# Dividing the side work of an attention loop over two steps, the PSUM bank held between them

## Chip, cores and metric

The kernel runs on one core of one Trainium2 chip. The metric is the device time of one execution in microseconds; lower is better. TensorE is called PE here, VectorE DVE, ScalarE ACT, GpSimd POOL and SyncE SP, as in the profile.

## What is computed

One layer of masked graph attention with residual norms, on x of shape (F, N, C) = (8, 2048, 256) with H = 8 heads of D = 32 channels, in float32:

```python
qkv = einsum('fnc,ck->fnk', x, w_qkv); q, k, v = split(qkv, 3)        # heads of 32
scores = einsum('fnhd,fmhd->fhnm', q, k) / sqrt(D)
attn = softmax(where(adj > 0, scores, -1e9), axis=-1)                 # adj is (2048, 2048), shared by all f and heads
t = einsum('fhnm,fmhd->fnhd', attn, v).reshape(F, N, C)
x1 = layernorm(x + t)
h = relu(einsum('fnc,cd->fnd', x1, w1) + b1)
x2 = layernorm(x1 + einsum('fnd,dc->fnc', h, w2) + b2)
out = layernorm(x + x2)
```

## The kernel before, in words

**The main loop.** `items` is a list of 8 x 4 x 2 x 16 = 1024 steps (f, qc, g, mb): graph copy f, a chunk qc of 512 queries, a group g of four heads, and a block mb of 128 keys. Sixteen steps with the same (f, qc, g) are called a group below. In step t the kernel first lets side work advance (`advance`), then issues `scores(items[t + LEAD])` with LEAD = 2, then `values(items[t])`, then `add_up(items[t])`.

- `scores` (lines 202 to 215) computes four heads' scores for one key block: four matmuls on PE into two PSUM tiles of two banks each (`score_pair`, three such pairs in turn, six banks), two DVE instructions that add the mask and write half of an SBUF tile `p` each (line 213), and one ACT instruction that takes the exponential of all of `p` in place (line 215).
- `values` (line 227) multiplies the four heads of `p` with V into the group's accumulator `O`, one PSUM bank that is held for the whole group. After the last block ACT copies it out as `oT` (line 231).
- `add_up` (lines 240 to 247) sums the `p` tiles of a group for the softmax's denominator. Blocks 0, 3, 6, 8, 11, 13, 15 are summed on POOL into block 0's tile (line 247); blocks 1, 4, 7, 10 and blocks 2, 5, 9, 12 are summed by two chains of accumulating DMAs, issued from POOL, into block 1's and block 2's tile (line 244); block 14 stands alone. So four tiles of a group stay alive until `denominator` has read them. The pool `pp` has 10 buffers for `p`.

**The PSUM banks.** Six of the eight banks hold scores. Of the other two (`ps_x`), one is the accumulator `O` of the group that runs, and the other, `1 - state["side"]`, is the single bank for all side work. The two change roles at each group's first step. No side work is issued in that step (`if mb: advance(t, 1)`).

**The side work.** Everything else is written as Python generators: `turn` (transposes x and makes the queries), `project` (keys and V), `turn_mask` (transposes the mask, first f only), `denominator` (sums `p` over keys by matmuls with ones, lines 271 to 295), `outcome` (transposes and scales the result, adds x by an accumulating DMA), and `tail` (norms, the two feed-forward matmuls `w1s` at line 339 and `w2s` at line 349, more norms, the store). They wait in the list `fill`, sorted by a due time written out by hand (`NEXT`, `start`). A generator yields a positive number to pause for so many steps, `TURNED`, `ROOM` or an `INPUTS` code to wait for a buffer, and `BANK` before it takes the side bank. `advance(t, 1)` walks the list in order of due time and lets one job pass its `BANK` in each step. All the matmuls up to the next `yield` are then issued at once; below, these are a *piece*. A piece ends with an instruction on ACT or DVE that empties the bank. The pieces of before are:

| piece | matmuls on PE | emptied by |
|---|---|---|
| transposes of `turn`, `tail` (`turnT`, `yT`, lines 157, 328) | 4 of 128x128 | ACT |
| transposes of `denominator`, `outcome` (`denT`, `outT`, lines 288, 311) | 4 of 128x128 | DVE |
| transposes of the mask (line 132) | 8 in bf16 | DVE |
| `chan`: a query or key chunk (`channels`, line 171) | 2 of 128x512 | ACT |
| `V` (line 192) | 8 of 128x128 | ACT |
| `den`, twice for each group (line 281) | 8 of 32x512 | ACT, after the second |
| `w1` (line 339) | 2 of 128x512 | ACT |
| `w2` (line 349) | 4 of 128x256 | DVE |

`denominator` is the one job that keeps the bank over two of its pieces: it yields `BANK` between them, and is by its due time the first in the list when it does. Its first piece becomes possible four steps after the group's last one (`start(t + SUM, ...)` with SUM = 4), that is at block 3 of the next group.

If the step's coming scores need a V chunk that doesn't exist yet, the loop calls `advance` again until it does.

Of the kernel before, what the change touches and what calls it, by code (L numbers as in the profile page):

```python
# [10 lines left out]
F32 = mybir.dt.float32  # L11
# [7 lines left out]
P = 128  # L19
H = 8  # L20
D = 32
CH = 512
# [3 lines left out]

SUM_MIN = 1e-25
SUM_MAX = 1e19
BANK, TURNED, ROOM, INPUTS = -1, -2, -3, -10

MASKED = -57344.0

# [21 lines left out]
def fast_path(ctx, tc, cst, x, adj, out, RS):  # L54
    nc = tc.nc
    F, N, C = x.shape
    NCK, TPC, MB = N // CH, CH // P, N // P
# [5 lines left out]
    kp = ctx.enter_context(tc.tile_pool(name="kp", bufs=2 * NCK + 2))  # L63
    qp = ctx.enter_context(tc.tile_pool(name="qp", bufs=2 * NCK + 2))
# [10 lines left out]
    ctx.enter_context(tc.manual_schedule())  # L75

    ident, identb, wqkv, w1s, w2s = cst["ident"], cst["identb"], cst["wqkv"], cst["w1s"], cst["w2s"]
    state = {"pair": 0, "side": None, "turn": 0, "turned": False, "tails": 0}

    def score_pair():  # L80
        i = state["pair"]
# [16 lines left out]
    def take(shape, dt):  # L98
        live.pop(0)
        live.append(ld.tile(shape, dt, name="in"))  # L100
        return live[-1]

    def give(t):
        live[:] = [None if u is t else u for u in live]
# [39 lines left out]
    QT, KT, V, XT = {}, {}, {}, {}  # L144
# [3 lines left out]
    def turn(f, c):  # L148
        yield INPUTS - 2
        xc, xT = take([P, TPC, C], F32), take([P, 2, CH], F32)  # L150
        nc.sync.dma_start(xc, x[f, c * CH:(c + 1) * CH, :].rearrange("(j p) c -> p j c", p=P))
        yield 3
        for a in range(2):
            yield BANK
            ps = bank()
            for j in range(TPC):
                nc.tensor.transpose(ps[:, j * P:(j + 1) * P], xc[:, j, a * P:(a + 1) * P], ident)
            nc.scalar.copy(xT[:, a, :], ps)
        give(xc)
        nc.sync.dma_start(XD[f][c], xT)  # L160
        XT[f, c] = xT
        yield 1
        for g in range(2):
            yield BANK
            QT[f, c, g] = channels(qp, "qT", xT, g * P)
        give(xT)

    def channels(pool, name, xT, k0):
        ps = bank()
        for a in range(2):  # L170
            nc.tensor.matmul(ps, wqkv[:, a, k0:k0 + P], xT[:, a, :], start=(a == 0), stop=(a == 1))  # L171
        t = pool.tile([P, CH], F32, name=name)
        nc.scalar.copy(t, ps)  # L173
        return t

    def project(f, c, g, xT=None):
        if xT is None:
            while (f, c) not in XT:
                yield 1
            yield INPUTS - 1  # L180
            xT = take([P, 2, CH], F32)
            nc.sync.dma_start(xT, XD[f][c])
            yield 3
            while len(KT) < (2 * f + g) * NCK + c:
                yield 1
        yield BANK
        KT[f, c, g] = channels(kp, "kT", xT, C + g * P)
        yield BANK
        ps = bank()
        for j in range(TPC):  # L190
            for a in range(2):
                nc.tensor.matmul(ps[:, j * P:(j + 1) * P], xT[:, a, j * P:(j + 1) * P],  # L192
                                 wqkv[:, a, 2 * C + g * P:2 * C + (g + 1) * P], start=(a == 0), stop=(a == 1))
        v = vp.tile([P, TPC, P], F32, name="v")
        nc.scalar.copy(v, ps.rearrange("p (j c) -> p j c", c=P))
        V[f, c, g] = v
        give(xT)
# [19 lines left out]
    LAST = MB - 1  # L217
# [53 lines left out]
    def denominator(f, qc, g):  # L271
        grp = (f, qc, g)
        terms = [PT.pop((f, qc, g, ALONE))] + [PT.pop((f, qc, g, chain[0])) for chain in MOVED + (POOLED,)]
        yield BANK
        ps = bank()
        for n, term in enumerate(terms):
            if n == 2:
                yield BANK
            for h in range(4):
                r = D * h  # L280
                nc.tensor.matmul(ps[r:r + D, :], cst["ones"], term[:, h, :], start=(n == 0), stop=(n == 3))  # L281
        dT = op.tile([P, CH], F32, name="dT")
        nc.scalar.copy(dT, ps)
        yield 1
        yield BANK
        ps = bank()
        for j in range(TPC):
            nc.tensor.transpose(ps[:, j * P:(j + 1) * P], dT[:, j::TPC], ident)
        if g == 0:
            RC[f, qc] = op.tile([P, TPC, H], F32, name="rc")  # L290
        rc = RC[f, qc]
        den = ps.rearrange("p (j c) -> p j c", c=P)[:, :, ::D]
        nc.vector.reciprocal(rc[:, :, 4 * g:4 * g + 4], den)
        nc.vector.tensor_tensor(RS[:, 0], RS[:, 0], den, ALU.add)
        nc.vector.tensor_tensor(RS[:, 1], RS[:, 1], den, ALU.min)
        if g == 1:
            begin = items.index((f, qc, g, LAST)) + SUM + 2
            start(begin, outcome(f, qc), begin)
# [20 lines left out]
    def tail(f, qc, y, xin):  # L319
        yield from norm(y)  # L320
        yield TURNED
        state["turned"] = True
        yT = work.tile([P, 2, CH], F32, name="turned")
        for a in range(2):
            yield BANK
            ps = bank()
            for j in range(TPC):
                nc.tensor.transpose(ps[:, j * P:(j + 1) * P], y[:, j, a * P:(a + 1) * P], ident)  # L328
            nc.scalar.activation(yT[:, a, :], ps, AF.Identity, bias=cst["be1c"][:, a:a + 1], scale=cst["g1c"][:, a:a + 1])
        yield 1  # L330
        nc.gpsimd.tensor_tensor(y, y, rows(cst["g1r"]), ALU.mult)
        yield 1
        nc.gpsimd.tensor_tensor(y, y, rows(cst["be1b2r"]), ALU.add)
        hT = work.tile([P, 2, CH], F32, name="hT")
        for d in range(2):
            yield BANK
            ps = bank()
            for a in range(2):
                nc.tensor.matmul(ps, w1s[:, a, d * P:(d + 1) * P], yT[:, a, :], start=(a == 0), stop=(a == 1))  # L339
            nc.scalar.activation(hT[:, d, :], ps, AF.Relu, bias=cst["b1s"][:, d:d + 1], scale=1.0)  # L340
        state["turned"] = False
        yield 1
        z = y
        for jj in range(0, TPC, 2):
            yield BANK
            ps = bank()
            for j in range(jj, jj + 2):
                for d in range(2):
                    nc.tensor.matmul(ps[:, (j - jj) * C:(j - jj + 1) * C], hT[:, d, j * P:(j + 1) * P], w2s[:, d, :],  # L349
                                     start=(d == 0), stop=(d == 1))  # L350
            nc.vector.tensor_tensor(z[:, jj:jj + 2, :], ps.rearrange("p (b c) -> p b c", c=C), z[:, jj:jj + 2, :], ALU.add)  # L351
        yield 1
        yield from norm(z)
        nc.gpsimd.tensor_tensor(z, z, rows(cst["g2r"]), ALU.mult)  # L354
        yield 1
        nc.gpsimd.tensor_tensor(z, z, rows(cst["be2r"]), ALU.add)  # L356
        yield 1
        nc.gpsimd.dma_start(z, xin, accum_op=ALU.add)
        yield 7
        yield from norm(z)  # L360
        nc.sync.dma_start(out[f, qc * CH:(qc + 1) * CH, :].rearrange("(p j) c -> p j c", p=P), z)
        state["tails"] -= 1


    fill = []

    def start(t, gen, due):
        fill.append([t, gen, 1, due])
        fill.sort(key=lambda e: e[3])

    def advance(t, banks):
        inputs = True
        for e in list(fill):
            while e[0] <= t:
                if e[2] == BANK:
                    if not banks:
                        break
                    banks -= 1  # L380
                elif e[2] < INPUTS:
                    inputs = inputs and not any(u is not None for u in live[:INPUTS - e[2]])
                    if not inputs:
                        break
                elif e[2] == TURNED and state["turned"] or e[2] == ROOM and state["tails"] == 2:
                    break
                e[2] = next(e[1], None)
                if e[2] is None:
                    fill.remove(e)
                    break  # L390
                if e[2] > 0:
                    e[0] = t + e[2]

    def mask_ahead(qc):
        for mc in range(NCK):
# [22 lines left out]
    for t, (f, qc, g, mb) in enumerate(items):  # L418
# [8 lines left out]
                due = t + MB // 2 if what is turn else items.index((f + 1, 0, which[1], which[0] * TPC)) - LEAD - 1  # L427
                start(t, what(f + 1, *which), due)
        if mb:
            advance(t, 1)  # L430
        if t + LEAD < len(items):
            nf, _, ng, nmb = items[t + LEAD]
            t0 = t
            while (nf, nmb // TPC, ng) not in V:
                advance(t0, 1)
                t0 += 1
            scores(items[t + LEAD])
        values(items[t])
# [3 lines left out]
    t = len(items)  # L442
    while fill:
        t += 1
        advance(t, 1)


@with_exitstack
# [233 lines left out]
```

## Time and profile before

| | us |
|---|---|
| median of 3 runs | 3766.22 (3762.61 to 3768.49) |
| the profiled execution | 3763.43 |
| its span | 3761.7 |
| PE busy | 3244.8 |
| DVE busy | 2761.9 |
| POOL busy | 2594.1 |
| ACT busy | 2412.1 |

The span runs from the first instruction to the last. A busy PE means that matmuls were in flight, not that PE was at its peak; matmuls overlap, so the times of single ones add to more than the busy time. The granted TensorE clock was 0.974 of full speed in the mean. The profile's chain of work that ended last covers 1% of the span here and says nothing of the loop; the loop is read from the timeline, the waits and the groups.

### The profile page before, as it was taken

To read this page: it belongs to the slowest core of one execution; us is meant where nothing else is said; L and a number is where in the kernel's file an instruction comes from. 1 tells how busy PE (TensorE), PEld (TensorE's weight loads), DVE (VectorE), ACT (ScalarE), POOL (GpSimd) and SP (SyncE) were. 2 spreads that over 40 slices of the span, in tenths; PEclk is the share of its full clock that TensorE was granted. 3 is DMA by queue.
4 is the path that set the end of the run, shared out by engine and by line. 5 is a ranking of instruction groups with operands and counts; after the bars stand their busy time and mean duration, and the time that the engine had idled before them with its cause. 6 is when DMAs were issued, how large, how long until landed. Compare 5 with 4: busy or idle time off the path is not lost. (4 is left out here: it accounts for less than half of the span.)

```text
span 3761.7 us, 53803 instructions
## 1 busy us (share of the span) xinstructions
PE 3244.8 (86%) x22020; PEld 1044.6 (28%) x22020; DVE 2761.9 (73%) x3207; ACT 2412.1 (64%) x1921; POOL 2594.1 (69%) x1355
## 2 busy tenths in 40 slices
PE   6778788988988989888998899888898888988884
PEld 4222223222322223222332223222232222322221
DVE  1886776777678776888667876787767777688882
ACT  2555655667667666666667765676766676677663
POOL 0555666677677776777757876677767777687775
PEclk8899999999999999999999999999999999999997
DMA  4665767677767767666757876766676676677663
GB/s 150 153 156 131 169 153 166 132 160 164 163 135 168 163 145 180 140 154 149 183 135 153 180 150 153 155 152 153 151 179 138 149 174 148 161 157 145 143 136 75
DMA packets 115181, 573.84 MB, mean 153 GB/s; under 512 B 11632, under 2 KB 29168, under 8 KB 61680
## 3 DMA queue, kind: packets, MB, share of 16 engines
q0 software_dynamic: 64512, 436.24, 57.6%
q1 hardware_dynamic: 48064, 132.13, 10.1%
q8 instruction: 174, 2.85, 0.3%
q10 hardware_dynamic: 2352, 1.97, 0.2%
q14 instruction: 79, 0.65, 0.1%
HBM read 129.90 MB, written 37.75 MB: 45 GB/s over the span
## 5 line engine op out<-in xcount | busy, mean ns | idle before, releaser
L213 DVE TENSOR_TENSOR p<-s,mask 128x1024 f32<-128x1024 f32 x2048 | 2408.8, 1218 | 751.4 <-PE s L210 482.0
L215 ACT ACTIVATE p<-p 128x2048 f32<-128x2048 f32 x1024 | 1957.0, 1911 | 1214.6 <-DVE p L213 878.9
L247 POOL TENSOR_TENSOR p<-p 128x2048 f32<-128x2048 f32 x384 | 1835.8, 4819 | 664.5 <-ACT p L215 656.2
L210 PE MATMUL s<-qT,kT 32*128 32x512 f32 x8192 | 1186.0, 649 | 236.3 <-DVE p L213 235.9
L227 PE MATMUL x<-p,v 128*32 128x512 f32 x8192 | 1110.0, 614 | 0.0
L244 POOL DMA_DIRECT2D p<-p x384 | 381.2, 1012 | 367.1 <-ACT p L215 143.6
L210 PEld LDWEIGHTS s<-qT,kT 32*128 32x128 f32 x8192 | 323.6, 185 | 855.9 <-DVE p L213 700.0
L227 PEld LDWEIGHTS x<-p,v 128*32 128x32 f32 x8192 | 162.1, 108 | 790.7 <-issue 629.9
L171 PE MATMUL x<-in,wqkv 128*128 128x512 f32 x476 | 238.0, 623 | 22.9 <-ACT oT L231 10.2
L265 ACT ACTIVATE y<-y,nb,rs 128x256 f32<-128x256 f32 x384 | 224.9, 589 | 39.9 <-POOL nb L262 39.9
L281 PE MATMUL x<-p,ones 128*32 128x512 f32 x2048 | 245.1, 597 | 2.3 <-DVE y L351 0.9
L254 DVE BATCH_NORM_STATS2 st<-y 128x6 f32<-128x256 f32 x384 | 159.8, 416 | 26.7 <-DMA y<-in_x_dram 26.7
L349 PE MATMUL x<-w2s,hT 128*128 128x256 f32 x512 | 129.4, 396 | 45.6 <-ACT oT L231 42.3
L339 PE MATMUL x<-turned,w1s 128*128 128x512 f32 x256 | 130.6, 633 | 20.7 <-ACT hT L340 19.3
L171 PEld LDWEIGHTS x<-in,wqkv 128*128 128x128 f32 x476 | 82.4, 192 | 185.5 <-issue 72.1
L192 PE MATMUL x<-wqkv,in 128*128 128x128 f32 x960 | 123.0, 281 | 6.4 <-ACT kT L173 6.3
L192 PEld LDWEIGHTS x<-wqkv,in 128*128 128x128 f32 x960 | 112.5, 192 | 57.4 <-ACT kT L173 34.0
L349 PEld LDWEIGHTS x<-w2s,hT 128*128 128x128 f32 x512 | 93.1, 192 | 113.4 <-ACT oT L231 68.6
L351 DVE TENSOR_TENSOR y<-x,y 128x512 f32<-128x512 f32 x64 | 44.2, 691 | 98.5 <-PE x L349 97.8
L281 PEld LDWEIGHTS x<-p,ones 128*32 128x32 f32 x2048 | 63.9, 110 | 165.8 <-issue 129.8
L259 POOL TENSOR_TENSOR rs<-rs,mhalf 128x4 f32<-128x4 f32 x96 | 99.3, 1035 | 8.0
L122 DVE TENSOR_SCALAR in<-in 128x1024 bf16<-128x1024 int32 x32 | 39.0, 1220 | 82.9 <-DMA in<-in_adj_dram 70.1
(69 smaller groups left out, 1422.6 us busy)
## 6 DMA issues: line engine op xcount, KB each, us to landing
p<-p POOLq DMA_DIRECT2D x384, 1024.0 KB, 9.7
y<-in_x_dram POOLq DMA_DIRECT2D x64, 512.0 KB, 6.1
in<-xd SPq DMA_DIRECT2D x60, 512.0 KB, 7.7
mask<-md SPq DMA_DIRECT2D x28, 1024.0 KB, 6.8
in<-in_x_dram SPq DMA_DIRECT2D x32, 512.0 KB, 6.6
xd<-in SPq DMA_DIRECT2D x32, 512.0 KB, 9.8
in<-in_adj_dram SPq DMA_DIRECT2D x32, 512.0 KB, 5.9
out_dram<-y SPq DMA_DIRECT2D x32, 512.0 KB, 3.1
```

What stands on the lines that cost most here:

```text
L171: nc.tensor.matmul(ps, wqkv[:, a, k0:k0 + P], xT[:, a, :], start=(a == 0), stop=(a == 1))
L192: nc.tensor.matmul(ps[:, j * P:(j + 1) * P], xT[:, a, j * P:(j + 1) * P], wqkv[:, a, 2 * C + g * P:2 * C + (g + 1) * P], start=(a == 0), s ...
L210: nc.tensor.matmul(ps2[half][:, j, :], KT[f, mb // TPC, g][r:r + D, (mb % TPC) * P:(mb % TPC + 1) * P], QT[f, qc, g][r:r + D, :], start=Tr ...
L213: nc.vector.tensor_tensor(pt[:, 2 * half:2 * half + 2, :], ps, MK[f, qc][:, mb, None, :].to_broadcast([P, 2, CH]), ALU.add)
L215: nc.scalar.activation(pt, pt, AF.Exp, scale=1.0 / math.sqrt(D))
L227: nc.tensor.matmul(O[grp][r:r + D, :], V[f, mb // TPC, g][:, mb % TPC, r:r + D], PT[item][:, h, :], start=(mb == 0), stop=(mb == LAST))
L244: nc.gpsimd.dma_start(PT[f, qc, g, chain[0]], PT.pop(item), accum_op=ALU.add)
L247: nc.gpsimd.tensor_tensor(first, first, PT.pop(item), ALU.add)
L254: nc.vector.bn_stats(st, t[:, j, :])
L265: nc.scalar.activation(t[:, j, :], t[:, j, :], AF.Identity, bias=nb[:, j:j + 1], scale=rs[:, j:j + 1])
L281: nc.tensor.matmul(ps[r:r + D, :], cst["ones"], term[:, h, :], start=(n == 0), stop=(n == 3))
L349: nc.tensor.matmul(ps[:, (j - jj) * C:(j - jj + 1) * C], hT[:, d, j * P:(j + 1) * P], w2s[:, d, :], start=(d == 0), stop=(d == 1))
```

## The change

The pieces `chan`, `V`, `den`, `w1` and `w2` get a point in their middle at which they yield a new code, `MORE`. At it the job keeps the bank and becomes the *holder*. At the end of each `advance`, if another job stands at its `BANK` and could have started, or if `finish` is asked for, the holder is resumed at once, so its second half is issued in the same step, as before. If nobody asks, the second half is left for the next step; there the holder is resumed first, and no other job may take the bank in that step (`free = False`). Between its two pieces `denominator` yields `HOLD` instead of `BANK`: the bank is kept over the step in any case, but a job that waits for it doesn't hasten it on. `finish` is set in a group's last step, in the loop that forces V chunks, and after the last step, so no bank is held when the two side banks change roles.

```diff
-BANK, TURNED, ROOM, INPUTS = -1, -2, -3, -10
+BANK, MORE, HOLD, TURNED, ROOM, INPUTS = -1, -2, -3, -4, -5, -10
...
-            yield BANK
-            QT[f, c, g] = channels(qp, "qT", xT, g * P)
+            yield from channels(QT, qp, "qT", (f, c, g), xT, g * P)
...
-    def channels(pool, name, xT, k0):
+    def channels(store, pool, name, key, xT, k0):
+        yield BANK
         ps = bank()
         for a in range(2):
+            if a:
+                yield MORE
             nc.tensor.matmul(ps, wqkv[:, a, k0:k0 + P], xT[:, a, :], start=(a == 0), stop=(a == 1))
-        t = pool.tile([P, CH], F32, name=name)
-        nc.scalar.copy(t, ps)
-        return t
+        store[key] = pool.tile([P, CH], F32, name=name)
+        nc.scalar.copy(store[key], ps)
...
@@ project, the V chunk @@
         for j in range(TPC):
+            if j == TPC // 2:
+                yield MORE
             for a in range(2):
...
@@ denominator @@
         for n, term in enumerate(terms):
-            if n == 2:
-                yield BANK
+            if n:
+                yield HOLD if n == 2 else MORE
...
@@ tail, w1 @@
             for a in range(2):
+                if a:
+                    yield MORE
...
@@ tail, w2 @@
             for j in range(jj, jj + 2):
+                if j > jj:
+                    yield MORE
...
-    def advance(t, banks):
+    def resume(e, t):
+        e[2] = next(e[1], None)
+        state["holder"] = e if e[2] in (MORE, HOLD) else None if state["holder"] is e else state["holder"]
+        if e[2] is None:
+            fill.remove(e)
+        elif e[2] > 0:
+            e[0] = t + e[2]
+
+    def advance(t, free=True, finish=False):
         inputs = True
+        if state["holder"]:
+            free = False
+            resume(state["holder"], t)
         for e in list(fill):
-            while e[0] <= t:
+            while e[2] is not None and e[0] <= t and e is not state["holder"]:
                 if e[2] == BANK:
-                    if not banks:
+                    if not free:
                         break
-                    banks -= 1
+                    free = False
...
-                e[2] = next(e[1], None)
-                if e[2] is None:
-                    fill.remove(e)
-                    break
-                if e[2] > 0:
-                    e[0] = t + e[2]
+                resume(e, t)
+        late = any(e[2] == BANK and e[0] <= t for e in fill)
+        while state["holder"] and (finish or late and state["holder"][2] == MORE):
+            resume(state["holder"], t)
...
         if mb:
-            advance(t, 1)
+            advance(t, finish=mb == LAST)
...
             while (nf, nmb // TPC, ng) not in V:
-                advance(t0, 1)
+                advance(t0, finish=True)
```

More of the change, by code (lines that the diff above doesn't have):

```diff
@@ L77, in fast_path @@
     ident, identb, wqkv, w1s, w2s = cst["ident"], cst["identb"], cst["wqkv"], cst["w1s"], cst["w2s"]
-    state = {"pair": 0, "side": None, "turn": 0, "turned": False, "tails": 0}
+    state = {"pair": 0, "side": None, "turn": 0, "turned": False, "holder": None, "tails": 0}
     def score_pair():
@@ L185, in project @@
                 yield 1
-        yield BANK
-        KT[f, c, g] = channels(kp, "kT", xT, C + g * P)
+        yield from channels(KT, kp, "kT", (f, c, g), xT, C + g * P)
         yield BANK
@@ L276, in denominator @@
         for n, term in enumerate(terms):
-            if n == 2:
-                yield BANK
+            if n:
+                yield HOLD if n == 2 else MORE
             for h in range(4):
@@ L444, in fast_path @@
         t += 1
-        advance(t, 1)
+        advance(t, finish=True)
 @with_exitstack
```

## The prediction

> **What bounds the kernel now.** I read the busy shares first, then the waits, then the timeline of single steps. The page's busy line says that PE leads without being full:
>
> ```profile
> PE 3244.8 (86%) x22020; PEld 1044.6 (28%) x22020; DVE 2761.9 (73%) x3207; ACT 2412.1 (64%) x1921; POOL 2594.1 (69%) x1355
> ```
>
> The groups and waits say what PE and DVE wait for (busy us, mean ns of one, idle before, releasers):
>
> ```profile
> L213 DVE TENSOR_TENSOR p<-s,mask 128x1024 f32<-128x1024 f32 x2048 | 2408.8, 1218 | 751.4 <-PE s L210 482.0
> L210 PE MATMUL s<-qT,kT 32*128 32x512 f32 x8192 | 1186.0, 649 | 236.3 <-DVE p L213 235.9
> L227 PE MATMUL x<-p,v 128*32 128x512 f32 x8192 | 1110.0, 614 | 0.0
> ```
>
> Scores wait for DVE and DVE waits for scores: the bound changes from step to step. The timeline shows a step without side work:
>
> ```profile
> 1609.25 1.14 PE L210 MATMUL s<-qT,kT 32*128 32x512 f32 x8 [0.41 <-DVE p L213]
> 1610.32 1.06 PE L227 MATMUL x<-p,v 128*32 128x512 f32 x8
> 1610.53 2.36 DVE L213 TENSOR_TENSOR p<-s,mask 128x1024 f32<-128x1024 f32 x2 [0.20 <-PE s L210]
> ```
>
> Scores hold PE for 1.07 us (1609.25 to 1610.32), values for 0.88 (elsewhere in the timeline, 1618.38 to a `den` piece at 1619.27), so PE needs 1.95. The step lasts 2.56, because the next scores need the PSUM pair that DVE is emptying. With a piece on PE the step is PE's. Taking each step from the first matmul of L227 to the next one, the usual length by piece is: none 2.56, `turnT` or `yT` 2.65, `outT` 2.75, `den` 3.78, `chan` and `w1` 3.98, `w2` 4.0, `V` 4.05. So a large piece costs 1.83 to 2.10 beyond 1.95, and an empty step leaves PE 0.61 idle.
>
> A second limit is the one side bank. In this stretch two transposes of `turn` stand in neighbouring steps:
>
> ```profile
> 1674.48 1.14 PE L210 MATMUL s<-qT,kT 32*128 32x512 f32 x8
> ...
> 1676.55 0.66 PE L157 MATMUL x<-ident,in 128*128 128x128 f32 x4
> ...
> 1678.08 1.91 ACT L215 ACTIVATE p<-p 128x2048 f32<-128x2048 f32 x1 [1.15 <-DVE p L213]
> ...
> 1679.90 0.57 ACT L158 COPY in<-x 128x512 f32<-128x512 f32 x1
> ...
> 1680.52 0.66 PE L157 MATMUL x<-ident,in 128*128 128x128 f32 x4 [1.24 <-ACT in L158]
> ```
>
> The first piece ends at about 1677.2. Its copy stands on ACT behind the exponential of the scores issued at 1674.48, which end 5.5 us after them. So the bank is free 6.04 us after those scores, however small the piece was. PE reaches the next piece 2 x 1.95 + p after them, p being the piece's own length: the wait is about 2.0 - p. It is 1.3 for p = 0.7 (the second transpose's step is 3.97, the first 2.65) and nothing for p = 2.0 (`chan` after `chan`: 3.98).
>
> **What the Trainium skill says.** "PSUM — Partial Sum Buffer", section "Engine vs sequencer instructions": ScalarE's, VectorE's and GpSimd's queues are strict FIFO, and matmuls start and complete in program order. The trace agrees: the copy above didn't pass the exponential, and PE stood 1.24 us at the piece with the scores behind it. "Perfetto Trace Analysis", section "Optimization Strategy": repeated gaps on an engine can mean that there is no buffer for the next tile. "DMA: Bandwidth & Descriptors", section "SWDGE vs HWDGE vs iDMA": accumulating DMAs can be issued from GpSimd only. So the two chains of sums share POOL's queue with its own sums; here their median from issue to landing is 9.7 us:
>
> ```profile
> DMA to landing us min/median/max: 6.8/9.7/14.7
> ```
>
> **The change, part by part.** The order in which both programs issue to PE gives the counts. No instruction is added or removed.
>
> (a) Filled steps. Steps without a piece fall from 338 to 204. Divided are 74 of 112 `chan`, 39 of 126 `den`, 14 of 56 `V`, 9 of 62 `w1` and 3 of 61 `w2`: 139. Four of them are paid back as steps with two pieces (a V chunk forced late), and one `w2` slips past the last step. Each divided piece turns 2.56 + (1.95 + p) into 2 x (1.95 + p/2): 0.61 less, as half a piece (2.9 to 3.0) lies above 2.56. 134 x 0.61 = **-82**. This is the bound if all the rest stays.
>
> (b) Bank waits. A half leaves p near 1.0 in its last step, so a piece in the very next step waits 2.0 - 1.0 = 1.0 where it waited 0 before. The order shows 83 such neighbours (60 after `chan`, 13 after `den`, 9 after `w1`, 1 after `V`): +83. Thirteen `den`-to-`denT` waits of 0.17, two pieces fewer at block 1 (1.5 each, behind `oT`'s copy) and a few transposes less give back 8. **+75**. Behind the waiting piece on PE stand the next scores, and DVE and ACT wait for those.
>
> (c) `p` buffers. Jobs that hold the bank push others back. `den` begins at block 3 in 62 of 63 groups before, and in only 26 after (17 at block 4, 17 at 5, 3 later); it ends at block 4 before, at 5 to 11 after. Until it has read them the old group's four tiles stay. Which place in SBUF each `p` gets shows the rest: before, from the second group on, a place is reused at the earliest 5 steps after (block 8 takes block 3's). After, block 6 takes block 3's place 37 times (3 steps), block 7 takes block 4's 20 times (3 steps), and some 30 more come at 3 or 4 steps after blocks 4 to 7. The sum of block 4 is a DMA. Laying the landing times of before's trace against its own mask adds, the adds would start before their place is free by 1.65 us in the mean for those 20, and by 86 in all; block 3's POOL sum is just in time (median 1.2 to spare). DVE is in order, so scores and exponentials stand behind such an add. The waits of (b) lengthen some of the same stretches, and a stall early in a group gives time to the later ones: I take half, **+45**, between 0 and 115 (all of it, and a bank wait after each third one).
>
> (d) Long empty steps. The mean of an empty step is 2.80, not 2.56, by norm work on DVE and stalls early in a group. Half pieces hide part of that: 134 x 0.24 = 32 at most, **-10** taken, between 0 and -32.
>
> (e) After the last step one `w2` more runs alone: **+3**, between 0 and 5.
>
> (f) Costed at nothing: the halves' own boundaries (matmuls still follow each other, with weights loaded ahead; bounded by a 0.1 change of weights, 139 x 0.1 = 14, and below by nothing); SP's loads and stores, which move by a few steps with the jobs (the `in` loads land in about 7 us and were given three steps); `outcome`'s DMA on POOL, issued up to four steps later: it had 13 to 15 us between landing and the first norm in most groups, four steps take about 12. If that cover goes, DVE waits at `st` (26.7 us, 4 times, before).
>
> Sum: -82 + 75 + 45 - 10 + 3 = +31 on the profiled 3763.4: 3794.4. The median of the runs stood 2.8 above the profiled execution: **3797**.
>
> **The rivals.**
>
> 1. The bank is free sooner after a half. ACT has 36% idle, and where the exponential is early the copy follows the half at once. The place is the 83 neighbours: below about 0.53 us each the sum falls under -7.5 and the change is faster. At 0.3 us and 20 in (c): -82 + 17 + 20 - 10 + 3 = -52, so 3714. Against it: the transposes' 1.24 us is measured on this bank, with the same ACT order.
> 2. The bank waits come as reckoned, but the sums are in time and (c) is nothing: -14, so 3752; with 15 in (c) it is no change. For it: before, DVE waited only 23.2 us for these DMAs. Against: before never reused a place within 3 steps in the loop's steady part.
> 3. The sums stall DVE in full, with bank waits after them: (c) = 115, so 3867. For it: POOL is 69% busy and its queue in order, and a chain's next DMA already waits for the one before (142.8 us).
> 4. The change doesn't divide much: excluded, the order shows 139 divided.
>
> **How the numbers follow.** About 0.2% (7.5 us) is what a measurement of this kernel can tell from no change. My case (3775 to 3840) has 0.50, the first rival 0.14, the second 0.21 (0.10 of it faster, 0.11 no change), the third 0.15. That gives faster 0.24, same 0.11, slower 0.65. The range for 8 in 10 runs from 3735 (part of rivals 1 and 2) to 3860 (most of rival 3).
>
> **What would show it.** Right: empty steps 204, half steps near 3.0; waits of PE's pieces for ACT's copies (`qT`, `kT`, `hT`, `dT`) up by some 75; DVE L213 waiting for DMA `p` and POOL L247 by tens of us, around blocks 7 to 10. Wrong: (b) if a piece after a half `chan` starts with less than 0.5 us of wait; (c) if L213's wait for DMA stays near 23; (a) if half steps take more than 3.2.

## The result, and the profile after

| | before | after |
|---|---|---|
| median of 4 runs, us | 3765.93 (3762.61 to 3768.49) | 3859.54 (3851.14 to 3861.88) |
| span of the profiled execution, us | 3761.7 | 3859.8 |
| mean granted TensorE clock | 0.974 | 0.967 |

The change makes the kernel slower: the ratio is 1.0245, 95% interval 1.0227 to 1.0263. The forecast was 3797 with a range to 3860: the sign was right, but the loss, 93.6 us, is three times the 31 of the forecast, and the time stands at the very edge of the range. The busy line of the page after:

```profile
PE 3274.4 (85%) x22020; PEld 1043.3 (27%) x22020; DVE 2764.7 (72%) x3207; ACT 2411.7 (62%) x1921; POOL 2594.9 (67%) x1355
```

The same work is done (all counts are the same), PE is busy 30 us longer and the span is 98 us longer. The groups of the page after (busy us, mean ns of one, idle before, releaser) show DVE waiting 100 us more before its mask adds (line 215, before 213), and PE waiting 10 us less before its scores:

```profile
L215 DVE TENSOR_TENSOR p<-s,mask 128x1024 f32<-128x1024 f32 x2048 | 2410.7, 1219 | 851.1 <-PE s L212 530.7
L212 PE MATMUL s<-qT,kT 32*128 32x512 f32 x8192 | 1198.2, 655 | 226.1 <-DVE p L215 224.8
L229 PE MATMUL x<-p,v 128*32 128x512 f32 x8192 | 1117.7, 618 | 0.0
```

Where the 98 us are is seen if PE's idle time in the trace is sorted by what PE starts next, and by whether the step has a piece:

| us | before | after | difference |
|---|---|---|---|
| PE busy | 3244.8 | 3274.4 | +29.6 |
| idle before a piece of side work | 225.5 | 300.5 | +75.0 |
| idle before scores, in a step with a piece | 29.7 | 82.3 | +52.6 |
| idle before scores, in an empty step | 206.6 | 143.8 | -62.8 |
| idle before the pieces after the last step | 18.8 | 22.7 | +3.9 |
| sum | | | +98.3 |

PE's idle time before the first and after the last matmul is not in the table; it is the same in both. So the empty steps gave 62.8 us, and two waits and PE itself took more than that back.

**The halves.** The timeline of the kernel after shows one `chan` in two steps (2090.05 and 2093.17), and the next job at the bank (2097.24):

```profile
2090.05 1.12 PE L173 MATMUL x<-in,wqkv 128*128 128x512 f32 x2 [0.21 <-ACT in L158]
2091.10 1.14 PE L212 MATMUL s<-qT,kT 32*128 32x512 f32 x8
2092.18 1.07 PE L229 MATMUL x<-p,v 128*32 128x512 f32 x8
2093.17 1.12 PE L173 MATMUL x<-in,wqkv 128*128 128x512 f32 x2
2094.23 1.14 PE L212 MATMUL s<-qT,kT 32*128 32x512 f32 x8
2094.81 1.91 ACT L217 ACTIVATE p<-p 128x2048 f32<-128x2048 f32 x1 [1.10 <-issue]
2095.30 1.06 PE L229 MATMUL x<-p,v 128*32 128x512 f32 x8
2096.62 0.57 ACT L175 COPY qT<-x 128x512 f32<-128x512 f32 x1
2097.24 1.13 PE L173 MATMUL x<-in,wqkv 128*128 128x512 f32 x2 [0.88 <-ACT qT L175]
```

From values (2092.18) to the half are 0.99 us where a `den` piece follows after 0.88, and from the half to the next scores are 1.06. A whole `chan` that doesn't wait has 0.99 and 1.91. So one matmul more costs 0.85, and entering and leaving a piece with 128x128 weights costs about 0.3 (0.11 before it, 0.2 after), once per half. The usual step with a half is 3.12, not the 2.96 that half of the piece would give; with half a `V` it is 3.16, with half a `w1` 3.12, with half a `den` 2.92.

The copy at 2096.62 stands behind the exponential of 2094.81, and the next piece waits 0.88 us for it: the wait that was forecast, at its place and nearly its size.

**The stalls.** One line of what ended DVE's idle time before its mask adds in after (us, times); it was 23.2, 19 before:

```profile
  DMA p<-p: 93.6, 40
```

Block 7 has 15 of these waits (49.2 us), block 9 has 14 (24.2), block 12 two (12.3). The longest at block 7 stands in the timeline so; block 4's accumulating DMA is issued at 1319.96 and lands at 1333.76, beside a store, a mask load and a load of x on SP's queue:

```profile
1319.91 0.34 SPq L367 DMA_DIRECT2D out_dram<-y  x1
1319.96 0.90 POOL L246 DMA_DIRECT2D p<-p  x1
1320.34 0.38 SPq L141 DMA_DIRECT2D mask<-md  x1
...
1320.82 0.67 SPq L151 DMA_DIRECT2D in<-in_x_dram  x1
...
1328.16 1.90 PE L283 MATMUL x<-p,ones 128*32 128x512 f32 x16
...
1333.88 2.36 DVE L215 TENSOR_TENSOR p<-s,mask 128x1024 f32<-128x1024 f32 x2 [7.27 <-DMA p<-p]
```

Block 7's `p` takes the place that block 4's held, so the mask add starts when that DMA is done; the second `den` piece at 1328.16 is the late one. But the late denominator is not all of it. The DMA shown took 13.8 us from issue to landing, where the same DMA took 6.9 in the kernel before. There the three transfers of SP started some 20 us ahead of it; here they start within 1 us of it. This happens in five groups in which block 7 takes block 4's place, one in each of f = 2 to 6: the DMA took 12.7 to 13.8 us, and these five waits are 33.9 of the 49.2. In five other such groups, with no transfer of SP beside it, the DMA took 7.1 to 7.2 and DVE was idle for 1.0 to 1.2 before block 7's mask add. That the transfers slowed the DMA is read from their coincidence; no run isolates it.

Block 9's waits have another origin. In 31 groups block 9 takes block 4's place, five steps after it; 12 of these wait, 23.2 us in all. In the kernel before, a place reused after five steps was block 3's, and block 3 is summed by an instruction on POOL and not by a DMA.

What PE does after the stall shown is in the timeline that follows:

```profile
1335.16 2.09 PE L212 MATMUL s<-qT,kT 32*128 32x512 f32 x8 [5.10 <-DVE p L215]
1337.18 1.93 PE L229 MATMUL x<-p,v 128*32 128x512 f32 x8
1339.04 1.13 PE L290 MATMUL x<-ident,dT 128*128 128x128 f32 x4
1340.10 1.50 PE L212 MATMUL s<-qT,kT 32*128 32x512 f32 x8
1341.53 1.07 PE L229 MATMUL x<-p,v 128*32 128x512 f32 x8
```

After 5.1 us without work PE takes 2.02 us for the scores and 1.86 for the values, twice the usual 1.07 and 0.88, and is back at its pace some 5 us later. This one stall costs PE about 2.7 us beyond its own length. The clock granted to PE was half in just this stretch. Each line has the stretch, its length, PE's busy time and instructions, the granted clock, and DMA's share and GB/s:

```profile
1256.00:1334.10 78.10, 66.74 (x449) 1.00 0.65 143
1334.10:1340.90 6.80, 5.74 (x24) 0.50 0.76 176
1340.90:1392.00 51.10, 44.28 (x340) 1.00 0.68 134
```

### The profile page after: what moved, and what is told of

Read it like the earlier page. It is cut to its first block, busy times and chain, and to the rows that moved or that the text cites. A ratio compares the mean times of both kernels' runs of the same rounds, so it can differ in the third digit from the quotient of the medians.

```text
span 3859.8 us, 53842 instructions
## 1 busy us (share of the span) xinstructions
PE 3274.4 (85%) x22020; PEld 1043.3 (27%) x22020; DVE 2764.7 (72%) x3207; ACT 2411.7 (62%) x1921; POOL 2594.9 (67%) x1355
## 5 line engine op out<-in xcount | busy, mean ns | idle before, releaser
L249 POOL TENSOR_TENSOR p<-p 128x2048 f32<-128x2048 f32 x384 | 1796.8, 4679 | 664.6 <-ACT p L217 659.2
L212 PE MATMUL s<-qT,kT 32*128 32x512 f32 x8192 | 1198.2, 655 | 226.1 <-DVE p L215 224.8
L246 POOL DMA_DIRECT2D p<-p x384 | 357.8, 987 | 380.8 <-ACT p L217 164.6
L173 PE MATMUL x<-in,wqkv 128*128 128x512 f32 x476 | 257.9, 640 | 46.8 <-ACT qT L175 15.7
L256 DVE BATCH_NORM_STATS2 st<-y 128x6 f32<-128x256 f32 x384 | 160.1, 417 | 45.1 <-DMA y<-in_x_dram 45.1
L360 POOL TENSOR_TENSOR y<-y,g2r 128x1024 f32<-128x1024 f32 x32 | 82.5, 2578 | 39.9 <-ACT y L267 36.8
L330 PE MATMUL x<-ident,y 128*128 128x128 f32 x256 | 45.6, 294 | 64.4 <-ACT turned L331 39.9
```

What stands on the lines that cost most here:

```text
L212: nc.tensor.matmul(ps2[half][:, j, :], KT[f, mb // TPC, g][r:r + D, (mb % TPC) * P:(mb % TPC + 1) * P], QT[f, qc, g][r:r + D, :], start=Tr ...
L246: nc.gpsimd.dma_start(PT[f, qc, g, chain[0]], PT.pop(item), accum_op=ALU.add)
L249: nc.gpsimd.tensor_tensor(first, first, PT.pop(item), ALU.add)
L256: nc.vector.bn_stats(st, t[:, j, :])
```

## The experiments

The theory: a filled step gains little, the side bank's late release costs about 75 us, and `p` tiles kept by late denominators cost the rest. Its rivals: the waits are not the bank's, the `p` places don't matter, or dividing costs by itself. Times are medians; each ratio is to runs of the kernel before on the same chip.

**1. Only the lateness.** The kernel before, nothing divided, the denominators two steps later:

```diff
-            start(t + SUM, denominator(f, qc, g), t)
+            start(t + SUM + 2, denominator(f, qc, g), t)
```

> The kernel before with one edit: each denominator job starts two steps later (block 5 and 6 instead of 3 and 4), nothing is divided. No step is filled or emptied (338 empty steps as before), so the filled-step gain is nil. Theory P (late denominators hold the four p tiles too long): blocks 6 and 7 now take the places of blocks 3 and 4 after 3 steps in all 63 groups, block 4's DMA sum is not done by then, so DVE's mask add waits for DMA p about 3.5 us in each group: 63 x 3.5 = 220, with overlap 100 to 220, and some 30 of bank waits because pieces become neighbours; 3890 to 4010 us. Rival R (only the bank waits matter): +30, 3797 us, and DVE's wait for DMA p stays near 23 us.

Measured: 4095.63 us, ratio 1.0854 (1.0828 to 1.0881), 329 us slower. DVE's mask adds wait for this, block 7 in 62 groups for 306.3 of it (4.9 each):

```profile
  DMA p<-p: 320.5, 81
```

Lateness alone, with no divided piece, costs more than the whole change (here block 7 takes block 4's place in all 63 groups, in after in 20). The rival falls. The cost is above the theory's 220 too: besides idle time (+166 before scores in steps with a piece, +70 before pieces) PE is busy 87 us longer, at a granted clock of 0.949. The timeline at one stall shows PE slow after it here as well:

```profile
447.21 2.35 DVE L213 TENSOR_TENSOR p<-s,mask 128x1024 f32<-128x1024 f32 x2 [7.00 <-DMA p<-p]
448.49 2.09 PE L210 MATMUL s<-qT,kT 32*128 32x512 f32 x8 [5.11 <-DVE p L213]
450.51 1.94 PE L227 MATMUL x<-p,v 128*32 128x512 f32 x8
```

**2. Only the denominator divided.** The kernel after without its other `yield MORE` lines.

> The kernel after, with only the denominator's pieces divided: chan, V, w1, w2 are whole. 49 den pieces are divided, empty steps fall from 338 to 289, denominators begin at block 3 in 61 of 63 groups and end at 4 to 6; the shortest reuse of a p place is block 3's, 4 steps later. A half den costs a step of 2.92, so a divided one gains 3.78 + 2.56 - 2 x 2.92 = 0.50: -25. Bank waits by neighbours +12. Theory P: no stall on p places: about -10, 3756 us. Rival (dividing costs of itself, by weight loads or the clock, whatever is divided): slower than before by 20 or more.

Measured: 3789.19 us, ratio 1.0057 (1.0039 to 1.0076), 22 us slower. The number is the rival's, the mechanism is not: PE is busy as long as before (3243.8) and half steps are 2.92 as expected. Empty steps gave 22 us; pieces wait 26 us more (12 expected) and scores in steps with a piece 21 more, with DVE's wait for DMA `p` at 48.1. I had expected no stall because block 4's place was reused after 3 steps only twice. But where the denominator ends at block 5 or 6, in 34 groups, block 9 takes block 4's place five steps after it, and 20 of these wait, 21.8 us in all: five steps were too few for a place that an accumulating DMA still read. By the trace, ten of the 22 us are in the first graph copy.

**3. All but the denominator divided.**

```diff
             if n:
-                yield HOLD if n == 2 else MORE
+            if n == 2:
+                yield BANK
```

> The kernel after, with the denominator as before (two whole pieces, the bank asked for twice): chan, V, w1, w2 divided (70, 20, 15, 3). Empty steps 235. Theory H (a half of a 128x128-weight piece costs 1.17, not 1.0: steps of 3.12): a divided chan gains 3.98 + 2.56 - 2 x 3.12 = 0.30 only, so filled steps give -32 in place of -63; bank waits +79; late denominators (10 reuses of block 4's place after 3 steps) 20 to 40: +70 to +90, 3835 to 3855 us. Rival: if dividing the denominator is the cost of the change, this is within 20 us of before.

Measured: 3821.61 us, ratio 1.0144 (1.0126 to 1.0163), 55 us slower, below the 70 to 90 expected. Half steps of `chan` are 3.12 and pieces wait 289.4 us (+64) as expected; the stalls are smaller than in after (DMA `p` 48.5). The trace is that of the fastest execution, 3810.10, so it shows about 12 us less than the median has. Of the change's parts this is the larger.

**4. Denominators on time.** The kernel after, but a piece begun in blocks 1 to 4 is finished in its step:

```diff
-            advance(t, finish=mb == LAST)
+            advance(t, finish=mb == LAST, whole=mb < 5)
...
-        while state["holder"] and (finish or late and state["holder"][2] == MORE):
+        while state["holder"] and (finish or (late or whole) and state["holder"][2] == MORE):
```

> The kernel after, but no MORE is left open in blocks 1 to 4 of a group (a piece begun there is finished in the same step), so that denominators begin at block 3 or 4 and only 3 reuses of block 4's place after 3 steps are left (20 in after). Empty steps 239. Theory P: filled steps -33, bank waits +70, place stalls near 10, so about 45 over before: 3811 us, some 50 under after, DVE's wait for DMA p back near 30 us (93.6 in after). Rival (place stalls don't matter): the difference to after is that of filled steps and waits alone, 20 us slower than after: 3880 us.

Measured: 3804.20 us, ratio 1.0106 (1.008 to 1.0132), 55 under after. The wait in question is nearly what it was before the change:

```profile
  DMA p<-p: 29.0, 17
```

Idle before scores in steps with a piece is 32.4 us (82.3 in after). With run 1 this shows the `p` places from both sides: lateness alone brings the stall, and taking lateness away removes most of it. Run 4 also leaves more pieces whole (239 empty steps where after has 204), so the 55 us are not the stalls' alone. What is left over before (+38) is the bank wait, 275.9 against 225.5, and the small gain of the halves.

**5 and 6. The bank freed by DVE after `chan` and `V`.** In both kernels:

```diff
-        nc.scalar.copy(store[key], ps)
+        nc.vector.tensor_copy(store[key], ps)
...
-        nc.scalar.copy(v, ps.rearrange("p (j c) -> p j c", c=P))
+        nc.vector.tensor_copy(v, ps.rearrange("p (j c) -> p j c", c=P))
```

> The kernel after, with the copies that empty the side bank after chan and V on DVE instead of ACT (192 copies). In DVE's queue such a copy stands behind one mask add, which ends 3.6 us after the scores, not behind the exponential, which ends 5.5 us after them. Theory B (the side bank's late release costs the change 60 of its 75 us of waits): PE's pieces no longer wait for copies of qT, kT, v (66 us in after), and this kernel stands 25 to 45 us over its own counterpart, the kernel before with the same copies on DVE; absolute about 3800 to 3820. Rival (the waits only move to the next cause, or the pieces wait for the exponential anyway): the distance to the counterpart stays near the 94 us of after to before.

> The counterpart: the kernel before, with the copies after chan and V on DVE. Whole chan and V pieces hardly wait for the bank (10.2 us for qT, under 1 for v), so both theories expect within 15 us of before, 3755 to 3780 us; DVE gains 192 x about 0.65 = 125 us of work, in steps where PE has the longer part.

Measured: 3800.09 us for the divided kernel (ratio 1.0076, 1.005 to 1.0102) and 3754.27 for its counterpart (0.996, 0.9948 to 0.9972): 46 us apart, where after and before are 94 apart. In after, PE's waits on these copies are lines like these (us, times, longest):

```profile
PE x L283 <- ACT kT L175: 17.4, 19, 1.2
PE x L194 <- ACT kT L175: 16.1, 16, 2.5
PE x L173 <- ACT qT L175: 15.7, 24, 0.9
```

In run 5 these three are gone (waits for DVE's copies in their place come to under 1 us), idle before pieces is 243.4 us against 224.0 in run 6, and idle before scores in steps with a piece stays at 82.5. So the copy's place behind the exponential on ACT was the cause of 56 of the 75 us of the first wait, and not of the second. What remains between runs 5 and 6 is the 19 us of bank waits, the stalls (idle before scores in steps with a piece, some 50 us more) and 43 us more of PE's busy time, less what the filled steps give; the stalls alone are not the 46 us.

**7. The undivided kernel's own short pieces.** The kernel before with the transposes of `turn` and `tail` emptied on DVE (`tensor_copy`, and `tensor_scalar` with a multiply and an add for `tail`).

> The kernel before, with the side bank emptied on DVE after the transposes of turn and tail (128 pieces of 0.7 us, the short pieces of the kernel before, which wait 43.6 + 45.9 us for ACT's copies). Theory B: these waits go, 70 to 85 us less: 3685 to 3700 us, faster than before and than after, with no piece divided. Rival (the exponential, not the bank, is what PE waits for, and the wait moves to the scores): within 20 us of before.

Measured: 3734.61 us, ratio 0.9898 (0.9866 to 0.993), 34 us faster; half of what was expected. The transposes' waits went, but part came back one piece later, at the `chan`, `V` and `w1` pieces that wait for ACT's copies of `qT` and `kT`. The PE waits of run 7:

```profile
PE x L171 <- ACT qT L173: 18.2, 27, 0.9
```

This wait was 3.2 us before; all waits of pieces for copies on line 173 rose from about 10 to 36.

**8 and 9. With both costs away.** Run 8 is run 4 with DVE emptying the bank after `chan`, `V`, the transposes and `den`; run 9 is the kernel before with the same copies and nothing divided.

> Division with its two costs taken away as far as a few edits can: denominators on time as in the run of that name (no piece left open in blocks 1 to 4), and the side bank emptied on DVE after chan, V, the transposes of turn and tail, and den. Theory: filled steps -33 on top of what the transposes' copies give (-75): 3655 to 3680 us, some 20 to 30 under the undivided kernel with the transposes on DVE. Rival: DVE, at about 83% of the span with its new copies, becomes the bound in half steps with norm work (2.4 + 0.7 + 0.6 us), and the divided kernel is no faster than the undivided one.

> The counterpart of the run with denominators on time and all copies on DVE: the kernel before, nothing divided, the side bank emptied on DVE after chan, V, the transposes of turn and tail, and den. Theory: with the bank waits away from both, division itself gains what the half steps gain, 33 us by step lengths, less some waits at block 1: this one stands 15 to 35 us above the divided one (3697), 3710 to 3735 us. Rival (the DVE copies made the whole gain and division adds nothing or costs): 3697 or less.

Measured: 3697.45 us (ratio 0.9809, 0.9783 to 0.9834) and 3694.03 (0.9805, 0.9777 to 0.9833): no difference. The copies made the whole gain, as the rival said, though not for its reason: DVE isn't the bound in half steps (3.12 as before). By the trace, the divided kernel is 4 to 10 us faster in each of the second to the seventh graph copy, 23 slower in the first and 15 in the last. Why in these two is not shown.

**10 to 12. Division only where it can gain.** Run 10 is run 8 with no open pieces in the first graph copy (`whole=mb < 5 or f == 0`). Run 11 also copies `oT` out on DVE. Run 12 is run 9 with that copy of `oT`.

> The divided kernel with all copies on DVE and denominators on time, but with no piece left open in the first graph copy (f = 0), whose steps took 506.8 us there and 485.6 in the kernel before. Theory: the first copy's mask work is bound by its inputs and gains nothing by division; 10 to 20 us come back: 3677 to 3690 us. Rival: the first copy's time is the DVE copies' and stays, within 5 us of 3697.

> The same, and the group's accumulator copied out (oT) on DVE as well. Every group's first side piece (block 1) waits for that copy behind an exponential, 1.5 us, 65 us in all. Theory: nearly all of it goes, 45 to 60 us less: 3625 to 3645 us. Rival: DVE is the bound there and the gain is under 20.

> The undivided counterpart with oT on DVE too. Theory: 50 us under the undivided one with oT on ACT, and 15 to 35 us above the divided kernel with oT on DVE. Rival: equal to the divided kernel or below it.

Measured: run 10 3674.31 us (ratio 0.9748, 0.9731 to 0.9764), 20 below run 9 on the same chip; run 11 3628.72 (0.9624, 0.9608 to 0.964); run 12 3642.57 (0.9659, 0.9641 to 0.9677), 14 above run 11; the two intervals lie side by side without overlap. So division kept out of the first graph copy and of blocks 1 to 4 is worth 14 to 20 us, about half a per cent, once the bank is free early. That is the low end of the 15 to 35 expected of it, or just under. The copy of `oT` gave 46 and 51 us, as expected. Run 11 is faster than before and after; nearly all of that is DVE's copies. The busy line of run 11:

```profile
PE 3245.2 (89%) x22020; PEld 1041.9 (29%) x22020; DVE 3039.2 (84%) x3655; ACT 2184.8 (60%) x1473; POOL 2595.0 (71%) x1355
```

## Why the prediction was right in sign and wrong in size

| step | forecast | measured | how measured |
|---|---|---|---|
| (a) filled steps, with the halves' boundaries of (f) | -82 | -49 | usual step lengths: empty 2.56, halves 3.12, 2.92, 3.16 |
| (b) bank waits | +75 | +75 | idle before pieces |
| (c) `p` buffers | +45 | +53 | idle before scores in steps with a piece |
| PE slow after a stall | not in the sum | +12 | scores and values over their usual length in steps with a piece, 28.4 us against 16.8 |
| (d) long empty steps | -10 | +4 | empty steps over 2.56: 81.0 us in all before, 84.6 after |
| (e) after the last step | +3 | +2 | from the last values to the end |
| sum | +31 | +97 | spans differ by 98 |

**(a) failed**, and is the largest miss: 33 of the 66 us that the sum lacked. I took half a piece as p/2, although p held a part that doesn't divide: the 0.3 us of entering and leaving. The trace of before had it to read: a `chan` of two matmuls costs 2.03, of which the two matmuls are 1.7. In (f) I bounded that boundary at 14 us for all pieces and took nothing. It is 0.3 for each divided `chan`, `V`, `w1` and `w2` (100 of them) and 0.1 for each of 39 `den`: 34 us. A divided `chan` gains 3.98 + 2.56 - 2 x 3.12 = 0.30, half of what was forecast. Run 3's half steps are 3.12 too. The sign named for a failure of (a), half steps over 3.2, didn't come: at 3.2 a divided `chan` would still gain 0.14 of the 0.61, so the sign was set too wide to see this.

**(b) was right** in cause and size: 0.88 us in the lines shown, 75.0 in sum, and moving the copies after `chan` and `V` to another engine takes 56 of it away (runs 5 and 6). By the copy waited for, `qT`, `kT` and `v` have 55 us more (61 forecast), `dT` 17 (13), `hT` 2 less (9 more).

**(c) was right in cause, and near in size partly by luck.** Runs 1 and 4 show the cause. But the size has two parts that the prediction left out. It counted places reused after 3 or 4 steps only, and 23.2 of DVE's 93.6 us of waits come from block 9 taking block 4's place after 5. And (f) put the moved loads and stores of SP at nothing, where the five slow DMAs beside them make 33.9 us of the waits. These two together are most of the 70 us by which DVE's waits for DMA `p` grew. (f) also put `outcome`'s DMA at nothing: DVE's wait for it at `st` rose from 26.7 us in 4 times to 45.1 in 10. The reading that `den` ends at block 5 to 11 in after is not quite right either: in nine groups it ends at block 4.

**The clock was missing.** By the records of the granted clock, PE ran at half clock in the loop in 21 stretches before, 31 in after and 60 in run 1, for 109, 177 and 341 us in all. The prediction had no term for this. The 68 us more in after can have cost 34 at most (an estimate: half of them, since the work done at half pace would have taken half as long). That this explains all of the 12 us in the table is worked out from the traces, not isolated by a run. PE's 30 us of busy time are these 12 and the boundaries of (a), less the end of a `values`, which counts as busy in an empty step and is covered by the piece in a filled one.

**(d) failed.** The time by which empty steps exceed 2.56 isn't carried by the steps that were filled. Much of it stands at block 0 of a group, where no side work is issued and so nothing can fill the step: 25.4 us of the 81.0 before, 36.9 of the 84.6 after.

Of the rivals, the first (bank free sooner) and the second (sums in time) fell. The third (stalls in full, 3867) had the number, but by luck: its stalls cost 115, where 53 and the clock's 12 were measured, and the true sum has less gain instead.

The Trainium skill's "PSUM — Partial Sum Buffer", section "Engine vs sequencer instructions", carried (b): strict order on ACT is what makes the copy late. "TensorE: Matmul & The Clock Gate", section "HAM oscillation — how this bites in real kernels", describes PE's clock falling when it waits, and that restarting is paid each time. The runs agree: scores of 2.02 us after a 5.1 us gap, and a mean clock of 0.974, 0.967 and 0.949 in before, after and run 1. The section speaks of idle gaps over about 3.4 us; in before 11 of the 21 half-clock stretches in the loop have no gap over 2.4 us in the 12 us ahead of them.

## What to carry to other kernels

Before dividing a piece to fill idle steps, split its length into what divides and what is paid at each entry, and ask what the piece holds while it is open: here a bank that is freed by a queue with a long instruction in it cost the neighbours more (about 0.9 us each) than the empty step was worth (0.61). A job that is delayed "because nobody asks" may itself be what others' buffers wait for: look at how many steps later each buffer's place is reused, before and after, and whether a DMA or an engine is the last to read it. Jobs that move take their transfers along: look at what these will run beside. Where a bank's release is late, try first to move the copy to the engine whose queue is short there; here that was worth far more than division.

## What the runs showed of the hardware that I had not expected

After an idle gap of 5.1 us PE worked at about half its pace for some 5 us (scores 2.02 us for 1.07, values 1.86 for 0.88), and the granted clock was 0.50 there; that stall cost PE about 2.7 us more than its length. Gaps of 1.8 to 2.4 us were followed by such stretches too. The mean granted clock went with the stalls in repeated runs: 0.972 to 0.976 in seven runs of before, 0.967 to 0.970 in four of after, 0.949 to 0.955 in four of run 1.

An accumulating DMA that took 6.9 us from issue to landing took 12.7 to 13.8 when a store, a mask load and a load of x were issued within 1 us of it.
